# Attention outputs of a gated cross-attention layer by Strassen's method over pairs of token tiles

## The chip, the cores and the metric

The kernel runs on one core of a Trainium2 chip. The metric is the device time of one execution in microseconds (us), as the median of several runs. A core has TensorE (PE, matrix multiplications and transposes), VectorE (DVE), ScalarE (ACT), GpSimd (POOL) and SyncE (SP, which issues DMAs), each with its own queue of instructions, which it works in order. PE writes to PSUM, which consists of banks of 512 floats in each of 128 partitions; DVE and ACT read the results from there.

## The reference

Everything is f32. A batch has 4 sequences of 1024 tokens with 512 features, 16 heads and 64 context rows per sequence.

```python
x = x + jnp.tanh(g_xattn[0]) * xattn(_layernorm(x), ctx_1024, ctx_1024, w_q, w_k, w_v, w_o)
x = x + jnp.tanh(g_ffn[0]) * ffn(_layernorm(x), w_gate, w_up, w_down)
# xattn
scores = jnp.einsum('bhqd,bhkd->bhqk', q, k) * SCALE       # causal mask added
weights = jax.nn.softmax(scores, axis=-1)
out = jnp.einsum('bhqk,bhkd->bhqd', weights, v)
return out.transpose(0, 2, 1, 3).reshape(bsz, q_len, HEADS * HEAD_DIM) @ w_o
# ffn: act_qdq rounds to 16 bits with one scale for the whole tensor, lpbq_dequant to 4 bits in blocks of 32
up = act_qdq(x @ lpbq_dequant(w_up).T)
gate = act_qdq(x @ lpbq_dequant(w_gate).T)
gate = act_qdq(gate * fixed_qdq_u16(jax.nn.sigmoid(gate)))
return act_qdq(gate * up) @ lpbq_dequant(w_down).T
```

The inner width of the feed-forward part is 1536. Only the attention part and the order of some weight preparation are touched by the change.

## The kernel before, in words

The 4096 tokens are 32 tiles of 128 tokens. Since the context has only 64 rows per sequence, the kernel folds the projections into two matrices per sequence: `m_all` (512 x 1024: key side times w_q, so that the scores of all heads are normalised x times it) and `vwo` (1024 x 512: value side times w_o, so that the attention output is the turned softmax weights times it). They are made in a setup stage of about 78 us; those of the sequences 2 and 3 go to DRAM and are fetched back later.

The attention stage is a loop over 16 pairs q of token tiles, four pairs to a sequence (about 78 to 560 us). A pair of its body does the following.

- It computes the scores of the next pair (`scores`, L524) by Strassen's method: seven products of a 2 x 2 block split, in which the two tiles are the block rows, instead of eight. Each product is two accumulating matmuls of 128x512, which the profile shows as four records (L536), in the three PSUM banks sp, sq, sn; ACT copies (L547, L553) and DVE additions (L542) put them together. The left factors' sums are made by DVE in `score_left` (L329), the right factors' sums once per sequence by DVE in `score_sums` (L347).
- `softmax` (L569) of these scores: a maximum (L580) and its negative (L590) on DVE, 16 exponentials per tile on ACT (L592, with a row sum each), the reciprocal (L597) and the product with it (L598) on DVE.
- `weights_turned` (L602) turns this pair's weights by PE transposes (L610) and ACT copies (L612).
- `renormed` (L631) takes tiles of two pairs earlier, whose attention is done: second layer norm (L637), maximum (L640), transposes (L645), copy on ACT (L646).
- `attend` (L615): per tile eight accumulating matmuls of 128x512 (one for each 128 of the contraction), which show as 16 matmul records (L621), as every f32 matmul here shows as two; then one DVE instruction x1 = tanh(g)*po + x (L627), a DMA of x1 to DRAM on POOL's queue (L628) and statistics for the second layer norm (L629).

From tile 16 on, chunks of w_gate are dequantized on DVE (`dequantized`, L211 to L222) and turned on PE (`turned_chunk`, L226), 12 chunks in 16 tiles (`gate_at`, L659). In the last eight tiles eight chunks of w_up are dequantized too, and turned behind the loop. Then come the gate stage (24 units of about 12.5 us), the up stage and the down stage, all of them with Strassen products; the gate stage dequantizes the four other chunks of w_up.

PE executes in the order in which the program is written (`tc.manual_schedule`). The order on the other engines is made by a scheduler from priorities, which follow the program's order; `tc.high_priority(SOON)` puts an instruction ahead. The built program's queues are then fixed. Big buffers are 20 slots of 8 KB; PSUM is three banks for scores, two for attention (`ps_o`, L521) and three for transposes (`ps_tr`).

Of the kernel before, what the change touches and what calls it, by code (L numbers as in the profile page):

```python
# [7 lines left out]
F32 = mybir.dt.float32  # L8
# [9 lines left out]
P = 128  # L18
# [9 lines left out]
def kernel(  # L28
# [38 lines left out]

    nc = tc.nc
# [30 lines left out]
    UPE = 8  # L99
# [165 lines left out]
    LO, HI = slice(0, HC // 2), slice(HC // 2, HC)  # L265
    add, sub = ALU.add, ALU.subtract
# [78 lines left out]
    score_right, t4m = {}, []  # L345

    def score_sums(b):  # L347


        m0, m1 = m_all[b]  # L350
        b11, b21, b12, b22 = m0[:, LO], m0[:, HI], m1[:, LO], m1[:, HI]
        t12 = slot([P, 2, HC // 2, H], f"t12m{b}")
        if b % 2 == 0:
            t4m.append(slot([P, 2, HC // 2, H], f"t4m{b // 2}"))
        t1, t2, t4 = t12[:, 0], t12[:, 1], t4m[-1][:, b % 2]
        score_right[b] = {1: b11, 2: b21, 3: b22, 4: t4, 5: t1, 6: t2, 7: b12}
        nc.vector.tensor_tensor(t1, b12, b11, sub)
        nc.vector.tensor_tensor(t2, b22, t1, sub)
        yield
        nc.vector.tensor_tensor(b12, b22, b12, sub)  # L360

        nc.vector.tensor_tensor(t4, b21, t2, sub)
        yield

    with tc.tile_pool(name="su", bufs=1) as su, tc.tile_pool(
# [130 lines left out]
        for a in reversed(range(B // 2)):  # L496
            if a == 0:
                for _ in score_sums(0):
                    pass
            for hp in range(HP):  # L500
                for b in (2 * a, 2 * a + 1):
                    ps = ps_mm.tile([P, H], F32, name=f"ps_vo{b}_{hp}", tag="mm")
                    for j in range(2):
                        half = slice(j * D, (j + 1) * D)
                        to = j if b % 2 == 0 else 1 - j
                        nc.tensor.matmul(
                            ps[to * D : (to + 1) * D, :], vT[half, hp, b * KL : (b + 1) * KL],
                            wo[hp // 4][half, hp % 4, :], start=True, stop=True,
                        )
                    dst = vwo[b][hp // 4][:, hp % 4, :]  # L510
                    if b % 2 == 0:
                        nc.scalar.copy(dst, ps)
                    else:
                        nc.vector.tensor_copy(dst, ps)
                    if b > 1 and hp % 4 == 3:
                        nc.gpsimd.dma_start(out=vwo_d[b][hp // 4], in_=vwo[b][hp // 4])


    xT = [None] * NTB
    with tc.tile_pool(name="ps_s", bufs=1, space=PSUM) as ps_s, tc.tile_pool(  # L520
        name="ps_o", bufs=2, space=PSUM  # L521
    ) as ps_o, tc.manual_schedule(engines={mybir.EngineType.PE}):

        def scores(q, then):  # L524


            a, b = left.pop(q), score_right[q // QPB]
# [5 lines left out]

            def prod(k, at, start):
                for h in range(HC // 2):
                    nc.tensor.matmul(  # L536
                        bank[at], a[k][:, h, :], b[k][:, h, :],
                        start=start and h == 0, stop=h == HC // 2 - 1, skip_group_check=True,
                    )

            def summed(dst, at, other):
                nc.vector.tensor_tensor(dst, bank[at], other, add)  # L542

            m1, c12, c22 = c[:, 1, 0], c[:, 0, 1], c[:, 1, 1]
            prod(1, "sp", True)
            with tc.high_priority(SOON):
                nc.scalar.copy(m1, bank["sp"])  # L547
            prod(6, "sq", True)
            with tc.high_priority(SOON):
                summed(c12, "sq", m1)  # L550
            prod(2, "sp", False)
            with tc.high_priority(SOON):
                nc.scalar.copy(c[:, 0, 0], bank["sp"])  # L553
            prod(7, "sq", False)
            with tc.high_priority(SOON):
                summed(c22, "sq", m1)
            prod(5, "sn", True)
            with tc.high_priority(SOON):
                summed(c22, "sn", c22)
            prod(4, "sq", False)  # L560
            with tc.high_priority(SOON):
                summed(m1, "sq", m1)
            then()
            prod(3, "sn", False)
            with tc.high_priority(SOON):
                summed(c12, "sn", c12)
# [35 lines left out]
        def weights_turned(t, e):  # L602

            ef = e[:, t % 2].rearrange("p h k -> p (h k)")
            eT = pa.tile([P, HP, P], F32, name=f"eT{t}", tag="eT")
            for q in range(HP // 4):
                ps = ps_tr.tile([P, 4, P], F32, name=f"ps_e{t}_{q}", tag="tr")
                for j in range(4):
                    hp = 4 * q + j
                    nc.tensor.transpose(ps[:, j, :], ef[:, hp * P : (hp + 1) * P], ident)  # L610
                with tc.high_priority(SOON):
                    nc.scalar.copy(eT[:, 4 * q : 4 * q + 4, :], ps)  # L612
                yield eT

        def attend(t, eT):  # L615

            b = t // TPB
            g, i = divmod(t, GRP)
            po = ps_o.tile([P, H], F32, name=f"po{t}", tag="po")
            for hp in range(HP):  # L620
                nc.tensor.matmul(  # L621
                    po, eT[:, hp, :], vwo[b][hp // 4][:, hp % 4, :],
                    start=(hp == 0), stop=(hp == HP - 1),
                )
            x1 = xg[g][:, i, :]
            with tc.high_priority(SOON):
                nc.vector.scalar_tensor_tensor(x1, po, tanh_g[0], x1, ALU.mult, ALU.add)  # L627
            nc.gpsimd.dma_start(out=x1_d[t], in_=x1)  # L628
            stats(pa, x1, mv2[:, t, :], f"b{t}")  # L629
# [26 lines left out]
        sg_t, ag, early_up = [], [], []  # L656
        last = NT - GRP

        gate_at = [NT // 2 + oc * (NT // 2) // IC for oc in range(IC)]  # L659
        gate_raw = {}  # L660
# [6 lines left out]

        two = centred(1)
        ahead = scores(0, lambda: next_left(1))
        softmax(0, ahead)  # L670
        for q in range(NQ):
            b, k = divmod(q, QPB)
            e = ahead
            if q % 2 == 0 and q // 2 + 2 < NG:
                load_group(q // 2 + 2)

            if b + 1 < B:
                if b > 0 and k == 0:
                    fetched(m_all[b + 1], m_d[b + 1], f"mb{b + 1}")
                if b > 0 and k == QPB - 1:  # L680
                    fetched(vwo[b + 1], vwo_d[b + 1], f"vb{b + 1}")
                if k == 1:
                    sums_ahead = score_sums(b + 1)
                if k in (1, 2):
                    next(sums_ahead)
            if q + 2 < NQ:
                two = centred(q + 2)
            if q + 1 < NQ:
                ahead = scores(q + 1, lambda: next_left(q + 2))
                softmax(q + 1, ahead)  # L690
            turns = [weights_turned(2 * q + i, e) for i in range(2)]
            next(turns[0])
            for i in range(2):
                t = 2 * q + i
                eT = next(turns[i])
                if q > 1:
                    renormed(t - GRP)
                if t in gate_at:
                    oc = gate_at.index(t)
                    turned_chunk(ps_tr, gate_raw.pop(oc), oc, wgT, "g")  # L700
                if i == 0:
                    next(turns[1])
                attend(t, eT)
                if t + AHEAD in gate_at:
                    oc = gate_at.index(t + AHEAD)
                    w = pa.tile([P, H], F32, name=f"w_g{oc}", tag="wraw", bufs=4)
                    dequantized(pa, w_gate[oc * P : (oc + 1) * P, :], w, f"g{oc}", oc < 4)
                    gate_raw[oc] = w
                if t >= NT - UPB:
                    ag.append(weight_sums(wgT, sg_t, t - (NT - UPB), "g"))  # L710

                if t >= last - GRP:
                    oc = t - (last - GRP)
                    if oc % GRP == 0:
                        w4 = slot([P, GRP, H], f"w_eu{oc // GRP}")
                    w = w4[:, oc % GRP, :]
                    dequantized(pa, w_up[oc * P : (oc + 1) * P, :], w, f"eu{oc}")
                    early_up.append(w)
                for c, d in ((0, 2), (2, 3), (3, 4)):
                    if t == last + d - 1:  # L720
                        w = slice(last + c, last + d)
                        rstd_of(pa, [(rstd2[:, w], mv2[:, w, 1])], f"c{c}")
# [8 lines left out]
        renormed(last + 1)  # L731
        renormed(NT - 2)
        for w in early_up[:-2]:
            up_chunk(ps_tr, w)
        renormed(NT - 1)
        for w in early_up[-2:]:
            up_chunk(ps_tr, w)
# [4 lines left out]
    with tc.tile_pool(name="praw", bufs=RAW) as praw, tc.tile_pool(  # L742
# [82 lines left out]
        with tc.tile_pool(name="pb", bufs=2) as pb, tc.tile_pool(  # L825
# [79 lines left out]
            w4 = slot([P, IC - UPE, H], "w_u4")  # L905
            ready = []
            for at, v in enumerate(tp * UPB + p for tp in pairs for p in range(UPB)):
# [5 lines left out]
                if at < IC - UPE:  # L913
                    oc = UPE + at
                    w = w4[:, at, :]
# [366 lines left out]
    def pair_steps(q, a):  # L1282
# [46 lines left out]
        LEFT, RIGHT = slice(0, HH), slice(HH, H)  # L1329
# [98 lines left out]
```

## Time and profile before

The time of the kernel is 1474.39 us (median of three runs, 1473.55 to 1474.7).

| | us |
|---|---|
| profiled execution | 1473.96 |
| its span | 1472.1 |
| PE busy | 1441.3 (98%) |
| DVE busy | 1090.3 (74%) |
| ACT busy | 639.4 (43%) |
| POOL busy | 95.5 (6%) |
| attention matmuls L621 (512 records, 593 ns mean) | 225.1 |
| exponentials L592 (480 records, 335 ns mean, without the reading of the sums) | 159.5 |

The profile is one execution. "Busy" is time in which an engine has an instruction in work; PE's instructions overlap, so that the mean duration of a matmul is longer than the distance between two starts, and it is this distance that counts. A timeline line gives start, duration, engine, line, output and inputs, the number of instructions taken together, and in brackets the idle time before the first of them with what ended it. The granted clock is 1.00 where TensorE runs at full speed.

### The profile page before, as it was taken

To read this page: it belongs to the slowest core of one execution; us is meant where nothing else is said; L and a number is where in the kernel's file an instruction comes from. 1 tells how busy PE (TensorE), PEld (TensorE's weight loads), DVE (VectorE), ACT (ScalarE), POOL (GpSimd) and SP (SyncE) were. 2 spreads that over 40 slices of the span, in tenths; PEclk is the share of its full clock that TensorE was granted. 3 is DMA by queue.
4 is the path that set the end of the run, shared out by engine and by line. 5 is a ranking of instruction groups with operands and counts; after the bars stand their busy time and mean duration, and the time that the engine had idled before them with its cause. 6 is when DMAs were issued, how large, how long until landed. Compare 5 with 4: busy or idle time off the path is not lost. (4 is left out here: it accounts for less than half of the span.)

```text
span 1472.1 us, 14498 instructions
## 1 busy us (share of the span) xinstructions
PE 1441.3 (98%) x4656; PEld 793.1 (54%) x4656; DVE 1090.3 (74%) x1986; ACT 639.4 (43%) x1653; POOL 95.5 (6%) x189
## 2 busy tenths in 40 slices
PE   8999999999999999999999999999999899999999
PEld 6544445444555454444444444444444448888887
DVE  3875657668777888999755569988888897666632
ACT  2536645655556663110011039977776432222200
POOL 0100000000000001000000000000000101111110
PEclk9999999999999999999999999999999999999999
DMA  8521212302122135652322439968557375555321
GB/s 300 226 90 51 79 71 72 136 32 75 51 104 70 77 130 210 247 218 101 138 85 99 159 115 337 374 231 304 211 213 268 144 292 182 186 186 174 141 72 43
DMA packets 71476, 231.67 MB, mean 157 GB/s; under 512 B 7268, under 2 KB 7524, under 8 KB 65892
## 3 DMA queue, kind: packets, MB, share of 16 engines
q1 hardware_dynamic: 46212, 131.09, 25.2%
q0 software_dynamic: 18272, 74.46, 13.0%
q10 hardware_dynamic: 6912, 25.17, 4.2%
q8 instruction: 36, 0.59, 0.2%
q14 instruction: 44, 0.36, 0.1%
HBM read 123.74 MB, written 106.95 MB: 157 GB/s over the span
## 5 line engine op out<-in xcount | busy, mean ns | idle before, releaser
L592 ACT ACTIVATE e<-e,mx 128x64 f32<-128x64 f32 x480 | 159.5, 335 | 12.6 <-DVE mx L590 12.5
L621 PE MATMUL po<-vwo,eT 128*128 128x512 f32 x256 | 112.6, 593 | 0.0
L621 PE MATMUL po<-vb,eT 128*128 128x512 f32 x256 | 112.5, 592 | 0.0
L765 PE MATMUL pqup<-t,wuT 128*128 128x512 f32 x192 | 92.4, 604 | 4.9 <-DVE raw_up L786 2.1
L592 ACT ACTIVATION_READ_ACCUMULATOR e<-e,mx 128x1 f32 x480 | 90.5, 189 | 0.0
L765 PE MATMUL pqgate<-t,wgT 128*128 128x512 f32 x192 | 90.4, 593 | 0.0
L781 ACT COPY raw_gate<-ppgate 128x512 f32<-128x512 f32 x24 | 14.1, 586 | 147.7 <-PE ppgate L765 147.7
L1294 PE MATMUL ep<-wdT,upe 128*128 128x256 f32 x336 | 77.1, 379 | 0.0
L621 PEld LDWEIGHTS po<-vwo,eT 128*128 128x128 f32 x256 | 47.4, 190 | 53.7 <-issue 53.6
L621 PEld LDWEIGHTS po<-vb,eT 128*128 128x128 f32 x256 | 47.4, 190 | 53.6 <-issue 53.6
L1220 ACT ACTIVATE uie<-upe,inv_up 128x1024 int16<-128x1024 f32 x48 | 53.6, 1145 | 46.4 <-DVE upe L1224 24.2
L1294 PE MATMUL eq<-tw,upe 128*128 128x256 f32 x312 | 72.4, 379 | 0.0
L1294 PEld LDWEIGHTS ep<-wdT,upe 128*128 128x128 f32 x336 | 63.8, 190 | 9.1 <-issue 0.5
L993 ACT ACTIVATE gi<-gt,inv_gate 128x1024 int16<-128x1024 f32 x48 | 54.9, 1143 | 30.6 <-DVE q L1003 30.3
L765 PE MATMUL ppgate<-xh,wgT 128*128 128x512 f32 x144 | 67.7, 592 | 0.0
L765 PE MATMUL ppup<-xu,wuT 128*128 128x512 f32 x144 | 67.7, 592 | 0.0
L765 PEld LDWEIGHTS pqup<-t,wuT 128*128 128x128 f32 x192 | 34.6, 189 | 57.1 <-issue 29.7
L1294 PEld LDWEIGHTS eq<-tw,upe 128*128 128x128 f32 x312 | 59.3, 190 | 8.1
L1224 DVE SCALAR_TENSOR_TENSOR upe<-uie,inv_o,gse 128x1024 f32<-128x1024 int16 (+1 forms) x50 | 60.5, 1235 | 3.0 <-ACT uie L1220 2.7
L765 PEld LDWEIGHTS pqgate<-t,wgT 128*128 128x128 f32 x192 | 36.2, 190 | 46.4 <-issue 38.5
L542 DVE TENSOR_TENSOR e<-sq,e 128x512 f32<-128x512 f32 x48 | 33.0, 688 | 36.8 <-PE sq L536 36.7
L893 DVE TENSOR_REDUCE am_gate<-raw_gate 128x1 f32<-128x1024 f32 x48 | 58.2, 1212 | 0.9
(330 smaller groups left out, 2881.6 us busy)
## 6 DMA issues: line engine op xcount, KB each, us to landing
gate_d<-raw_gate ACTq DMA_DIRECT2D x48, 512.0 KB, 2.6
gt<-gate_d SPq DMA_DIRECT2D x48, 512.0 KB, 4.7
upe<-up_d SPq DMA_DIRECT2D x24, 1024.0 KB, 6.5
up_d<-raw_up POOLq DMA_DIRECT2D x46, 512.0 KB, 3.6
gse<-gsi_d SPq DMA_DIRECT2D x24, 512.0 KB, 4.0
gsi_d<-q SPq DMA_DIRECT2D x44, 256.0 KB, 4.0
xg<-in_x_dram SPq DMA_DIRECT2D x8, 1024.0 KB, 6.3
x_d<-xg POOLq DMA_DIRECT2D x32, 256.0 KB, 2.3
```

What stands on the lines that cost most here:

```text
L542: nc.vector.tensor_tensor(dst, bank[at], other, add)
L592: nc.scalar.activation(ei[:, h, :], ei[:, h, :], AF.Exp, bias=mx[:, h : h + 1], accum_out=sm[:, h : h + 1],)
L621: nc.tensor.matmul(po, eT[:, hp, :], vwo[b][hp // 4][:, hp % 4, :], start=(hp == 0), stop=(hp == HP - 1),)
L765: nc.tensor.matmul(bank[at], a[k][:, h, :], b[k][:, h, :], start=start and h == 0, stop=h == HC // 2 - 1, skip_group_check=True,)
L781: nc.scalar.copy(r0[:, 0, :], bank["pp"])
L893: nc.vector.tensor_reduce(am_gate[:, u : u + 1], rf, AX.X, ALU.max, apply_absolute_value=True)
L993: nc.scalar.activation(gi, g, AF.Copy, scale=inv_g)
L1220: nc.scalar.activation(ui, up[:, i, :], AF.Copy, scale=inv_u)
L1224: ins = nc.vector.scalar_tensor_tensor(o[:, i, w], ui[:, w], c_o, gs[:, i, w], ALU.mult, ALU.mult)
L1294: nc.tensor.matmul(bank[at], a[u // 2][k][:, u % 2, q % 2, :], w_of[u // 2][k][:, u % 2, :], start=start and u == 0, stop=u == UPB - 1, sk ...
```

## The change

The attention output of a pair is now computed by Strassen's method as the scores are: the weights of the two tiles are the block rows, the contraction (1024) and the output width (512) are halved. Seven products of four program matmuls (56 records of 128x256) take the place of two tiles of 16 records of 128x512.

- The left factors' sums (four additions of 128x512 per pair) are made by POOL in `weights_turned`, which now turns a pair at a time, between the score products.
- The right factors' sums of `vwo` are made once per sequence by `batch_sums`, which replaces `score_sums`; all of them run on POOL, but for the scores' first.
- The tanh factor is multiplied into `vwo` when it is copied out of PSUM.
- The first product is copied by ACT (r); the others are added by DVE in 128x256 quarters straight to the two tiles of x, and POOL adds r to the other quarters. Two of the three accumulators are halves of one PSUM tile ("opn"), the third has a bank.
- The score products are done in the order 1, 6, 2, 5, 7, 3, 4 with the turning of weights behind 5 and 3.
- Gate chunks are turned from tile 20 on, two per pair ahead of `attend` in pairs 10 to 13, and the last four behind the loop; four early up chunks instead of eight are made ready in the loop, and the gate stage makes eight. The loads of tile groups are issued later in the body, and sums of gate weights start two tiles later.

```diff
-    UPE = 8
+    UPE = 4
@@
+    def batch_sums(b, k, engine):
+        if k == 0:
+            m0, m1 = m_all[b]
+            b11, b21, b12, b22 = m0[:, LO], m0[:, HI], m1[:, LO], m1[:, HI]
+        else:
+            v0, v1 = vwo[b]
+            b11, b12, b21, b22 = (v[:, :, h] for v in (v0, v1) for h in (LEFT, RIGHT))
...
+        engine.tensor_tensor(t1, b12, b11, sub)
+        engine.tensor_tensor(t2, b22, t1, sub)
         yield
-        nc.vector.tensor_tensor(b12, b22, b12, sub)
-        nc.vector.tensor_tensor(t4, b21, t2, sub)
+        engine.tensor_tensor(b12, b22, b12, sub)
+        engine.tensor_tensor(t4, b21, t2, sub)
         yield
@@
-                        nc.scalar.copy(dst, ps)
+                        nc.scalar.activation(dst, ps, AF.Copy, scale=tanh_g[0])
                     else:
-                        nc.vector.tensor_copy(dst, ps)
+                        nc.vector.tensor_scalar(dst, ps, tanh_g[0], None, ALU.mult)
@@
-        name="ps_o", bufs=2, space=PSUM
+        name="ps_o", bufs=1, space=PSUM
@@
+        def weights_turned(q, e):
+            eT = pa.tile([P, 7, HP // 2, P], F32, name=f"eT{q}", tag="eT", bufs=1)
+            for i in range(2):
+                ef = e[:, i].rearrange("p h k -> p (h k)")
+                for k in range(2):
+                    ps = ps_tr.tile([P, 4, P], F32, name=f"ps_e{q}_{i}_{k}", tag="tr")
...
                 with tc.high_priority(SOON):
+                        nc.scalar.copy(eT[:, 2 * i + k], ps)
...
+            a11, a12, a21, a22, s1, s2, s4 = (eT[:, k] for k in range(7))
+            nc.gpsimd.tensor_tensor(s1, a21, a22, add)
+            nc.gpsimd.tensor_tensor(s2, s1, a11, sub)
+            nc.gpsimd.tensor_tensor(a21, a11, a21, sub)
+            made.append(nc.gpsimd.tensor_tensor(s4, a12, s2, sub))
+            yield {1: a11, 2: a12, 3: s4, 4: a22, 5: s1, 6: s2, 7: a21}
+
+        def attend(q, a):
...
+            for k, at, start, dst in (
+                (1, "op", True, None), (6, "oq", True, x1[:, RIGHT]), (2, "op", False, x1[:, LEFT]),
+                (5, "on", True, x2[:, RIGHT]), (7, "oq", False, x2[:, RIGHT]),
+                (3, "on", False, x1[:, RIGHT]), (4, "oq", False, x2[:, LEFT]),
+            ):
+                for h in range(HP // 2):
+                    nc.tensor.matmul(
+                        bank[at], a[k][:, h, :], b[k][:, h, :],
+                        start=start and h == 0, stop=h == HP // 2 - 1, skip_group_check=True,
+                    )
                 with tc.high_priority(SOON):
-                nc.vector.scalar_tensor_tensor(x1, po, tanh_g[0], x1, ALU.mult, ALU.add)
+                    if k == 1:
+                        nc.scalar.copy(r, bank[at])
+                    else:
+                        nc.vector.tensor_tensor(dst, bank[at], dst, add)
+                if k == (6 if last else 3):
+                    engine.tensor_tensor(x1[:, RIGHT], x1[:, RIGHT], r, add)
+                if k == (2 if last else 4):
+                    v = x2.rearrange("p (n h) -> p n h", n=2)
+                    engine.tensor_tensor(v, v, r.unsqueeze(1).to_broadcast([P, 2, HH]), add)
...
+                behind = {3: lambda: next_left(q + 2)}
+                if q > 0:
+                    behind = {5: turn, 3: lambda: (a.append(turn()), next_left(q + 2))}
+                ahead = scores(q + 1, behind)
                 softmax(q + 1, ahead)
...
+            for t in (2 * q, 2 * q + 1):
+                oc = t - gate_from
+                if 0 <= oc < IC - 4:
+                    turned_chunk(ps_tr, gate_raw[oc], oc, wgT, "g")
+            attend(q, a[0])
+            if b + 1 < B and k in (1, QPB - 1):
+                with tc.issue_after(made[-1].ins):
+                    for _ in batch_sums(b + 1, k // 2, nc.gpsimd):
+                        pass
```

## The prediction

> **What bounds the kernel now.** I read, in this order, the engine totals, the table of stretches, the order of TensorE's work in one pair of token tiles, and then what the other engines hold ready for it. "L" numbers are lines of the kernel before, "A" numbers lines of the changed one.
>
> ```profile
> PE 1441.3 (98%) x4656; PEld 793.1 (54%) x4656; DVE 1090.3 (74%) x1986; ACT 639.4 (43%) x1653; POOL 95.5 (6%) x189
> ```
> ```profile
> 200.00:300.00 100.00, 99.84 (x309) 49.31 (x308) 66.82 (x137) 63.67 (x287) 4.90 (x10) 1.00 0.28 103
> ...
> 400.00:500.00 100.00, 99.99 (x339) 51.76 (x339) 82.33 (x177) 58.41 (x240) 3.79 (x7) 1.00 0.23 82
> ```
>
> In the second fence the columns are length, PE, PEld, DVE, ACT, POOL busy, then the granted clock. The pairs run from about 78 to 560 us; in these stretches PE is never idle, so less PE work is worth its full time, and so is each new PE wait, because no other slack stands ahead of it. DVE is at 67 to 82 of 100 and ACT at 55 to 64: both have room on average, but each works its queue strictly in order.
>
> ```profile
> 245.00 1.88 PE L536 MATMUL sq<-m_all,xs 128*128 128x512 f32 x4
> ...
> 251.02 1.88 PE L536 MATMUL sn<-m_all,xs 128*128 128x512 f32 x4
> 252.74 1.04 PE L610 MATMUL ps_e<-ident,e 128*128 128x128 f32 x8
> 253.61 0.60 PE L645 MATMUL ps_xm<-ident,xm 128*128 128x128 f32 x4
> 254.08 0.66 PE L610 MATMUL ps_e<-ident,e 128*128 128x128 f32 x4
> 254.57 7.03 PE L621 MATMUL po<-vwo,eT 128*128 128x512 f32 x16
> ```
>
> Starts give the prices, since PE's ends overlap: a score product (4 matmuls) is 252.74-251.02 = 1.72 us; 8 transposes 253.61-252.74 = 0.87; 16 attention matmuls end 6.87 us after they start (261.44-254.57), 0.429 each of 512 columns. An attention tile in before needs one DVE instruction after it, and two PSUM buffers alternate, so that nothing on PE waits for it.
>
> ```profile
> 256.67 0.35 ACT L592 ACTIVATE e<-e,mx 128x64 f32<-128x64 f32 x1 [1.18 <-DVE mx L590]
> 257.01 0.33 ACT L592 ACTIVATE e<-e,mx 128x64 f32<-128x64 f32 x1
> ```
> ```profile
> 261.64 0.75 DVE L627 SCALAR_TENSOR_TENSOR xg<-po,tg,xg 128x512 f32<-128x512 f32 x1 [4.94 <-PE po L621]
> 262.31 0.24 DVE L597 RECIPROCAL rs<-sm 128x16 f32<-128x16 f32 x1
> ...
> 263.04 1.21 DVE L598 TENSOR_TENSOR e<-e,rs 128x1024 f32<-128x1024 f32 x1
> ...
> 267.89 0.25 DVE L597 RECIPROCAL rs<-sm 128x16 f32<-128x16 f32 x1 [3.56 <-ACT e L592]
> ```
>
> The exponentials run one per 0.333 us, 16 per tile: 5.33 us, both tiles 10.7. DVE stands still for 3.56 us at 267.89 for the last of them. Today nothing on PE is behind that; this is the place to watch.
>
> **The saving.** Attention goes from 2x16 matmuls of 512 columns per pair to 7x8 of 256. A 256-column matmul in the down stage (L1294) starts every 0.216 us (12 in 2.59 us). So 56x0.216 = 12.09 us for 32x0.429 = 13.74: 1.65 us per pair, x16 pairs = -26.5 us. The transposes stay. Four fewer early up chunks at the end (16 transposes, 1.7 us) return in the gate stage, and cancel.
>
> **What moves off or on.** DVE per pair: six additions from PSUM of 128x256 (0.422 each, L1326) for two of 0.748: +1.0 us. The per-batch score sums leave DVE (4x1.22 for three batches, -14.6 us in all). ACT: one more 128x256 copy, 0.37 (L1308). The tanh scale goes into the copies of the value matrices: nothing, they run on ACT and DVE either way. Four more dequantizations of about 2.85 us go into the gate stage: 11.4 us of DVE, behind 24 units of 12.5 us of PE there; weights were ready 7 us or more ahead of use, so 0, and at most 11.4 without that cover. SP's loads of the next two tile groups are issued a pair later, but their slots are read a pair after that still: 0.
>
> **New waits on PE.** Let T be the end of score product 3. After T the changed order has 8 transposes of the second weight tile, 8 of the next x, score product 4 and 8 transposes of the renormalized tiles: attention starts at T+0.87+0.87+1.72+0.87 = T+4.33, its products (each 1.73) end at 6.06, 7.78, 9.51 and so on.
> (1) Products 2 and 5 are in the two halves of one PSUM tile ("opn"), and the built program has the first matmul of product 5 wait for DVE's reading of product 2 just before. DVE starts some 0.2 after the last matmul, needs 0.42, PE restarts 0.1 later: 0.7 us, in each pair: 11.5 us. With nothing else ahead in DVE's queue that is the whole loss.
> (2) Something is ahead in it. In the changed order of DVE, on odd pairs the reciprocal (A591) and the 1.22 us product (A592) of the first tile stand before that reading. Their exponentials can start at T+3.1 (the score row's maximum and ACT's four copies of 0.59 go first), take 5.33 and share ACT with the new copy (0.37): reciprocal done at T+9.1, product 6's reading 0.42, A592 1.22, the reading 0.42: 11.2, against 9.51 on PE: 1.7, or 2.6 where the mask's 1.2 us comes first, 2.9 in pair 1. I take 2.2 for pairs 3, 5, 7, 9. On even pairs a 0.68 maximum (A671) comes between: 1.0 to 1.6, I take 1.3 (with a 1.28 us table load on ACT). Pairs 1 to 9: 2.9+4x2.2+4x1.3 = 16.9.
> (3) Pairs 10 to 13 carry two gate chunks each ahead of attention, not one in 1.33 tiles. The second chunk's transposes need a buffer of the three in "ps_tr", which ACT's copy of a renormalized tile frees (A677). In pairs 12 and 13 that copy is behind all 32 exponentials in ACT's queue: 3.1 (4.4 with the table load of pair 12)+10.7+0.6 = T+14.4 to 15.7, then 0.5 of transposes, against an attention start of T+5.2 with the chunks. That is 9.7 and 11, and with (1) and the dequantizations on DVE ahead of its readings 10.4 and 13. In pair 10 the second tile's reciprocal (after 32 exponentials) is ahead of product 2's reading: 8.9; in pair 11 dequantizations hold the exponentials up: 5.9. Below, these four cannot be under 20 us, unless ACT's exponentials are quicker than 0.333; above, DVE adds some 8.
> (4) The first pair (POOL's sums of the value matrices right before use) 2.7, pair 14 0.8, pair 15 2.5.
> Sum: 16.9+8.9+5.9+13+10.4+2.7+0.8+2.5 = 61.1, which includes (1). Before had 4.4 us of gaps in the pairs: +56.7.
>
> **POOL.** Per pair it gets four 128x512 additions of turned weights, one 128x256 and one 128x512 addition to x, and per batch eight of 128x1024. No POOL row of this kind exists. From below: DVE's 128x512 addition took 0.69 (L219). From above a page: the Trainium skill, GPSIMD Engine Reference, section Elementwise — side-by-side cycle accounting, has an addition of 2048 floats at 4497 ns, as an estimate 2.2 ns an element: 1.15 us. The second sum, s2, is for product 6. The copies end at about T+1.9: s2 is there at T+1.9+2x0.69 = 3.3 or T+1.9+2x1.15 = 4.2, and product 6 starts at 6.06. By either nothing is lost; I take the page's, no row of POOL being near. Against the change stands another rule, the Trainium skill, SBUF — State Buffer, section Who interferes with whom: a DVE instruction with two SBUF inputs and a POOL instruction that reads SBUF shut each other out. DVE's sums of x parts (4x0.418, L342) and its products e*rs (2x1.22) have two SBUF inputs and fall there. The row: POOL did 95.5 us in all before, mostly issuing DMAs, and shows nothing of it. By the row 0; by the rule a sum waits for one such instruction at most, 1.2 us each: s2 at 4.2+2x1.2 = 6.6, 0.5 us late, 8 us over 16 pairs. I take 0 for the likeliest, since most of DVE's work beside s2 reads PSUM or one input, and keep 8 for the range.
>
> **The clock.**
>
> ```profile
> 341.46 1.31 PE L335 MATMUL ps_xn<-ident,xn 128*128 128x128 f32 x8 [2.61 <-DVE xn L323]
> ```
> ```profile
> 341.00:352.00 11.00, 10.54 (x42) 6.23 (x43) 9.64 (x18) 5.94 (x14) 0.00 (x0) 0.84 0.08 25
> ```
> After a gap of 2.61 us the granted clock averaged 0.84 over 11 us: (1-0.84)x11 = 1.7 us lost (the matmul of four at 342.56 took 3.39 for 1.88). Gaps of 1.56 and 1.28 at 568 and 571 left it at 1.00. The Trainium skill, TensorE: Matmul & The Clock Gate, section "What's actually happening", has a free-running window of 3.4 us. A rule of 3.4 us idle would charge only pairs 10 to 13, 4x1.7 = 7; the row charges from 2.6 us on, some 6 gaps (those four, pair 1 and one of the odd ones), 6x1.7 = 10 us. By the rule the sum below would be 3 us less; I take the row's 10.
>
> **Sum.** 1474.0 (profiled execution; span 1472.1) -26.5+56.7+0.7 (end of attention: two chunks' sums behind the last tile)+10 = 1514.9. The median is 0.4 above the profiled execution: 1515.
>
> **Rivals.**
> (A) Faster: ACT and DVE run far enough ahead that only the 0.7 us bank wait stays. 1474.4-26.5+11.5-4.4 = 1455; with the clock untouched. It asks that the copies A677 in pairs 12 and 13 aren't behind the exponentials in time; deciding point: losses under 31 us in total. For it: DVE has 18 to 33% idle. Against: both queues' order is fixed.
> (B) Half the waits of (2) to (4) and little of the clock: 11.5+25-4.4-26.5+4 = +10 to +20: 1484 to 1495.
> (C) POOL is the bound: additions over 2.1 us each (or shut out by DVE) bring s2 past product 6's start (2x2.1+1.9 = 6.1). At 3 us each it is 1.8 late per pair, +29: 1544. Against: twice DVE's price is 1.4.
> (D) The saving isn't there: 256-column matmuls could stand on their weight loads (190 ns each, L1294). The down stage's 0.216 speaks against.
>
> **How the numbers follow.** Chance of the forecast (1500 to 1530) 0.50, B 0.25, C 0.15, A 0.08, D within the others 0.02. 1485 leaves out A and a little of B, 1548 the worse half of C. Faster by over 0.2% (about what a measurement of this kernel tells from no change) 0.08, within 0.02, slower 0.90.
>
> **What would show it.** In the trace after: A643 matmuls 0.216 us apart (saving); a PE gap of 0.7 us or more ahead of product 5 in each pair, released by DVE xg A651; 1.3 and 2.2 us alternating; gaps of about 10 us ahead of the gate transposes of pairs 12 and 13, released by ACT xT A677; clock under 1 after them; no gap released by POOL outside the first and last pairs. It is wrong if POOL's additions take over 2 us, or the gaps at pairs 10 to 13 are under 3 us.

## The result, and the profile after

The changed kernel takes 1563.62 us (median of 4 runs, 1561.32 to 1564.24) against 1473.97 for the kernel before (4 runs): 1.0608 times as long, 95% interval 1.0589 to 1.0626. The prediction, 1515 with a range up to 1548, had the direction and most of the places right, but less than half of the size: 41 us of 90.

The engine totals of the changed kernel, to be read against those of before:

```profile
PE 1444.9 (93%) x5040; PEld 882.7 (57%) x5040; DVE 1159.2 (74%) x2034; ACT 646.8 (41%) x1668; POOL 287.7 (18%) x311
```

PE's busy time did not fall although 26.5 us of matmuls left it, and its share is 93% where it was 98%. Two stretches of the changed kernel say why (columns: length, PE, PEld, DVE, ACT, POOL busy, granted clock, DMA share, GB/s):

```profile
200.00:300.00 100.00, 88.53 (x351) 60.19 (x350) 72.14 (x130) 53.04 (x230) 48.65 (x34) 0.97 0.22 79
...
400.00:500.00 100.00, 75.97 (x301) 52.38 (x299) 81.24 (x139) 48.18 (x208) 44.50 (x30) 0.87 0.20 74
```

PE stands still for 11 of 100 us in the one and 24 in the other, in stretches where it was idle for 0.2 us or less before, and the granted clock falls to 0.97 and 0.87 (1.00 before). Busy time at a lower clock counts as busy: that hides the saving in the totals.

The account of the attention stage: from the first score matmul to the first gate matmul the time grew from 489.7 us (78.40 to 568.09) to 578.0 (79.55 to 657.51), by 88.3 us. I added up PE's gaps over 0.08 us in both: 7.0 before, 95.7 after. Without gaps this part is 482.7 and 482.3 us long, the same, although the saving of 26.5 and four up chunks (1.7) are gone from it. So something took back 28 us: 88.3 = 88.7 (gaps) - 28.2 (work) + 27.8. Most of it is the clock: 1 minus the granted clock, summed over the time in which PE works in this stage, is 25.4 us in the changed kernel's trace and 1.7 in the one before; some 4 us of the 27.8 stay unexplained.

One even pair of the changed kernel, PE's timeline (start, duration, instruction; in brackets the idle time before it and what ended it):

```profile
173.24 1.89 PE L643 MATMUL opn<-vwo,eT 128*128 128x256 f32 x8
174.97 1.89 PE L643 MATMUL oq<-t,eT 128*128 128x256 f32 x8
177.16 1.99 PE L643 MATMUL opn<-vwo,eT 128*128 128x256 f32 x8 [0.30 <-ACT r L649]
182.01 2.98 PE L643 MATMUL opn<-t,eT 128*128 128x256 f32 x8 [2.86 <-DVE xg L651]
184.78 2.64 PE L643 MATMUL oq<-vwo,eT 128*128 128x256 f32 x8
187.26 1.89 PE L643 MATMUL opn<-vwo,eT 128*128 128x256 f32 x8
```

The products are 1.73 us apart where nothing waits (174.97-173.24), as predicted. Product 5 (182.01) waits for DVE's reading of product 2, as predicted, but 2.86 us and not 1.3; then two products take 2.77 and 2.48 us, at a lower clock. What DVE did meanwhile:

```profile
171.76 0.46 DVE L341 TENSOR_TENSOR xs<-xs 128x256 f32<-128x256 f32 x1
172.14 1.24 DVE L584 TENSOR_SCALAR mx<-mx 128x16 f32<-128x16 f32 x1
173.30 1.56 DVE L325 TENSOR_SCALAR xn<-xg,mv,rstd 128x512 f32<-128x512 f32 x1
174.78 1.48 DVE L342 TENSOR_TENSOR xs<-xs 128x256 f32<-128x256 f32 x1
176.19 0.68 DVE L558 TENSOR_TENSOR e<-sq,e 128x512 f32<-128x512 f32 x1
```

and POOL beside it:

```profile
170.68 1.26 POOL L613 TENSOR_TENSOR eT<-eT 128x512 f32<-128x512 f32 x1 [9.75 <-ACT eT L609]
172.01 1.34 POOL L614 TENSOR_TENSOR eT<-eT 128x512 f32<-128x512 f32 x1
173.31 1.27 POOL L615 TENSOR_TENSOR eT<-eT 128x512 f32<-128x512 f32 x1
174.54 1.45 POOL L616 TENSOR_TENSOR eT<-eT 128x512 f32<-128x512 f32 x1
```

The negation of 16 maxima takes 1.24 us (0.17 when nothing runs on POOL, and in the kernel before, L590), the normalisation 1.56 (0.54), the sum of x parts 1.48 (0.42). Each ends within 0.3 us of the end of a POOL addition: 173.38 against 173.35, 174.86 and 174.58, 176.26 and 175.99. These are 3.1 us by which DVE is late for product 6 and product 2, and 2.1 of them are instructions with a single input (negation and normalisation).

DVE instructions that read one of two inputs from PSUM, and reductions (L574, 1.21 us with POOL at work and without), are not held up. One that runs wholly beside a POOL addition, DVE first, then POOL:

```profile
412.73 0.41 DVE L651 TENSOR_TENSOR xg<-opn,xg 128x256 f32<-128x256 f32 x1
```
```profile
411.68 3.33 POOL L369 TENSOR_TENSOR mb<-mb 128x1024 f32<-128x1024 f32 x1
```

Beside the sums made once per sequence (128x1024, 2.3 to 3.3 us on POOL) it is worse; here DVE in pair 11, while POOL makes such sums:

```profile
482.76 2.06 DVE L342 TENSOR_TENSOR xs<-xs 128x256 f32<-128x256 f32 x1
484.74 2.55 DVE L343 TENSOR_TENSOR xs<-xs 128x256 f32<-128x256 f32 x1
487.22 2.56 DVE L344 TENSOR_TENSOR xs<-xs 128x256 f32<-128x256 f32 x1
489.70 2.71 DVE L584 TENSOR_SCALAR mx<-mx 128x16 f32<-128x16 f32 x1
```

ACT's first exponential starts behind these at 492.50, the copy of product 1 (r), which is in ACT's queue behind four of the exponentials, at 493.85, and PE waited 11.50 us for it.

### The profile page after: what moved, and what is told of

Read it like the earlier page. It is cut to its first block, busy times and chain, and to the rows that moved or that the text cites. A ratio compares the mean times of both kernels' runs of the same rounds, so it can differ in the third digit from the quotient of the medians.

```text
span 1561.9 us, 15489 instructions
## 1 busy us (share of the span) xinstructions
PE 1444.9 (93%) x5040; PEld 882.7 (57%) x5040; DVE 1159.2 (74%) x2034; ACT 646.8 (41%) x1668; POOL 287.7 (18%) x311
## 3 DMA queue, kind: packets, MB, share of 16 engines
q0 software_dynamic: 18272, 74.46, 12.3%
## 5 line engine op out<-in xcount | busy, mean ns | idle before, releaser
L556 ACT COPY e<-sp 128x512 f32<-128x512 f32 x32 | 18.7, 584 | 153.4 <-PE sp L550 153.4
L643 PE MATMUL opn<-t,eT 128*128 128x256 f32 x128 | 42.1, 485 | 39.2 <-DVE xg L651 39.2
L1009 POOL DMA_DIRECT2D up_d<-raw_up x46 | 24.5, 532 | 257.0 <-ACT si L1042 116.6
L643 PE MATMUL oq<-t,eT 128*128 128x256 f32 x256 | 61.0, 381 | 3.3 <-POOL eT L614 3.3
L550 PE MATMUL sq<-t,xs 128*128 128x512 f32 x128 | 61.9, 607 | 0.5 <-DVE xs L342 0.5
L643 PE MATMUL opn<-vb,eT 128*128 128x256 f32 x192 | 50.4, 409 | 11.8 <-ACT r L649 11.8
```

What stands on the lines that cost most here:

```text
L550: nc.tensor.matmul(bank[at], a[k][:, h, :], b[k][:, h, :], start=start and h == 0, stop=h == HC // 2 - 1, skip_group_check=True,)
L556: nc.scalar.copy(dst, bank[at])
L643: nc.tensor.matmul(bank[at], a[k][:, h, :], b[k][:, h, :], start=start and h == 0, stop=h == HP // 2 - 1, skip_group_check=True,)
L1009: queue.dma_start(out=up_d[u], in_=raw[u])
```

## The experiments

Each is an edit of the changed kernel, whose time is 1563.62 us; ratios are to the kernel before, which ran beside each, with 95% intervals. In the text, "lock" is short for this: an instruction of DVE or POOL stands still while one of the other engine runs.

**POOL writes the sums without reading.** The sums of factors are left out and zeros stand in their place; POOL's additions to x stay, and read.

```diff
-            nc.gpsimd.tensor_tensor(s1, a21, a22, add)
+            nc.gpsimd.memset(s1, 0.0)
...
-        engine.tensor_tensor(t1, b12, b11, sub)
+        engine.memset(t1, 0.0) if engine is nc.gpsimd else engine.tensor_tensor(t1, b12, b11, sub)
```

> Leaves out the sums of factors on POOL (those of the turned weights, of the value matrices and of the later score matrices): POOL fills the same buffers with zeros instead, so it writes SBUF and does not read it; PE's order, and DVE's order in pairs 1 to 9, are as in the changed kernel. Theory of the lock (a DVE instruction with two SBUF inputs, or a copy-like one, stands still while a POOL addition runs): DVE's x sums return from up to 2.6 us to 0.42 and the negated maxima (A584) from 1.2-2.7 to 0.16, the gaps ahead of product 5 in pairs 1 to 9 fall from 2.9-4.9 us to 0.9-2.3, pair 11's gap of 11.5 to about 3, and the total by 9x2+9 of gaps and some 12 of clock: about 1525. Pairs 12 and 13 keep their 10 to 12 us. Theory of the queue order alone (what stands ahead of the readings costs what it cost before): DVE's durations and the gaps stay, 1555 to 1565.

Measured: 1503.51 us, ratio 1.0196 (1.0179 to 1.0213): 60 us less, some 22 more than expected. The groups of this kernel (busy us, mean ns, idle before):

```profile
L344 DVE TENSOR_TENSOR xs<-xs 128x256 f32<-128x256 f32 x16 | 6.7, 419 | 0.0
...
L584 DVE TENSOR_SCALAR mx<-mx 128x16 f32<-128x16 f32 x30 | 6.0, 201 | 0.4
```

and of the changed kernel:

```profile
L344 DVE TENSOR_TENSOR xs<-xs 128x256 f32<-128x256 f32 x16 | 15.2, 949 | 0.0
...
L584 DVE TENSOR_SCALAR mx<-mx 128x16 f32<-128x16 f32 x30 | 22.1, 736 | 0.4
```

In pairs 1 to 9, where DVE works the same instructions in the same order but for seven swaps of neighbours, it has its old durations back, and the gaps ahead of product 5 are 0.52 us in every even pair and 0.9 to 1.9 in odd ones, 9.2 us in nine pairs for 34.1. Pair 11's loss goes from 12 us to 1.4; pairs 12 and 13 keep 12.3 and 9.3. POOL's fills are also shorter than its additions (0.54 us against 1.3), but in these pairs PE waited for no POOL result in either kernel, and the 14 of DVE's x sums that ran beside a fill took 0.42 or 0.43 us all the same: for the instructions with two inputs in SBUF it is the reading that hurts. (The negation of maxima was held up by fills too, three times, for 0.3 us each.) This settles the lock as a cause; the order of the queues explains what is left.

**The order of the products.**

```diff
-                (5, "on", True, x2[:, RIGHT]), (7, "oq", False, x2[:, RIGHT]),
-                (3, "on", False, x1[:, RIGHT]), (4, "oq", False, x2[:, LEFT]),
+                (7, "oq", False, x2[:, RIGHT]), (5, "on", True, x2[:, RIGHT]),
+                (4, "oq", False, x2[:, LEFT]), (3, "on", False, x1[:, RIGHT]),
```

> Only the order of the attention products is changed, to 1, 6, 2, 7, 5, 4, 3, so that one product lies between each reading of a PSUM half and the product that needs it. Theory of the bank wait: each of 15 pairs gains up to 1.7 us of cover, the gaps of 2.9 to 4.1 ahead of product 5 shrink to 1.2 to 2.4, the granted clock is restored in those pairs (about 1 us each more): 1563 - 24 - 12, about 1525 to 1535. Rival (DVE is late as a whole, the wait only moves to the next product): 1555 to 1565.

Measured: 1538.93 us, ratio 1.0443 (1.0425 to 1.0460): 24.7 us less, where 28 to 38 were expected. Now each product waits for a reading two products back, so that 1.7 us of PE's own work covers it. In odd pairs waits of 1.3 to 1.4 us stayed ahead of product 5, and others moved to product 7 (0.4 to 1.8 us); on balance the gaps of the attention stage fell from 95.7 to 81.1 us, and its time without gaps from 482.3 to 468.6: half of the gain is clock (25.4 us lost in the changed kernel, 12.3 here).

**Gate chunks behind attention.**

```diff
-            for t in (2 * q, 2 * q + 1):
-                oc = t - gate_from
-                if 0 <= oc < IC - 4:
-                    turned_chunk(ps_tr, gate_raw[oc], oc, wgT, "g")
             attend(q, a[0])
+            for t in (2 * q, 2 * q + 1):
+                oc = t - gate_from
+                if 0 <= oc < IC - 4:
+                    turned_chunk(ps_tr, gate_raw[oc], oc, wgT, "g")
```

> Only the gate chunks of pairs 10 to 13 are turned behind attention instead of ahead of it. Theory (their transposes wait for ACT's copy of a renormalized tile, which is behind 32 exponentials): the gaps of 12.2 and 10.7 us in pairs 12 and 13 go, with 3 to 7 us of clock; pair 11's 11.5 us stays, since it comes from POOL's sums: about 1533 to 1540. Rival (the lateness moves to ACT's copy r or to the next pair): 1555 to 1565.

Measured: 1539.33 us, ratio 1.0443 (1.0425 to 1.0460): 24.3 us less. The gap that it removes, as the changed kernel's PE and ACT show it:

```profile
536.39 1.11 PE L227 MATMUL wps_g<-ident,w_g 128*128 128x128 f32 x4 [12.15 <-ACT xT L677]
```
```profile
535.45 0.33 ACT L586 ACTIVATE e<-e,mx 128x64 f32<-128x64 f32 x1
...
535.78 1.04 ACT L677 COPY xT<-ps_xm 128x512 f32<-128x512 f32 x2
```

The copy that frees the PSUM buffer comes right behind the last exponential, as the prediction said. In pairs 12 and 13 the chunks' waits are gone; 2.7 and 3.0 us ahead of products 2 and 5 come out in their place. The gaps of the stage fell by 24 us, the whole gain: the 3 to 7 us of clock that were expected with them did not come, but pair 11's wait, which was to stay, fell by 3 us.

**All sums of factors on DVE.**

```diff
-            nc.gpsimd.tensor_tensor(s1, a21, a22, add)
+            nc.vector.tensor_tensor(s1, a21, a22, add)
...
-                    for _ in batch_sums(b + 1, k // 2, nc.gpsimd):
+                    for _ in batch_sums(b + 1, k // 2, nc.vector):
```

> All sums of factors go from POOL to DVE, where they stand in its queue at 0.69 us (four per pair) and 1.22 us (eight per sequence). Theory of the lock: DVE loses about as much time to its own additions (2.75 us a pair) as it lost standing still for POOL's (2 to 3), so pairs without batch sums change little, and those with them gain some 2 us, pair 11 more: 1540 to 1560. If POOL were merely late with its results (its 1.3 us an addition on PE's path), the gaps would close: under 1530. If DVE's queue were the only trouble, four more instructions ahead of the readings would make it slower: over 1575.

Measured: 1514.53 us, ratio 1.0285 (1.0265 to 1.0305): 49 us less. My range for the lock, 1540 to 1560, was missed; the number falls into the one that I had set for a POOL that is merely late with its results. That isn't the cause all the same: in the changed kernel PE waited for a POOL sum in two pairs only, for 1.83 (pair 0) and 1.48 us (pair 15). With four more additions a pair in its queue DVE was still earlier than beside POOL: product 5 waited 0.9 to 1.8 us in pairs 1 to 9, not 2.9 to 4.9. The engine that was to be relieved is better off with the work: an addition costs it 0.68 us (L613) in its own queue, while POOL needs 1.3 us for it and can hold DVE up for all of that.

**Only the sums per sequence on DVE**, the pair's four stay on POOL (the second line of the diff above alone, and the same for the first sequence; as in that run, these sums no longer have to wait for the pair's).

> One part undone: the sums made once per sequence go from POOL to DVE (1.22 us each there), POOL keeps the four sums of turned weights. Theory of the lock: the odd pairs lose the part of their gaps that came with POOL's 2.3 to 3.3 us instructions (1 to 2 us each, with clock), pair 11's 11.5 us shrinks to 3 to 5: 1540 to 1550, and the even pairs keep 2.9 us each. Rival (eight more DVE instructions per sequence hold the readings up as long): 1560 or more.

Measured: 1562.47 us, ratio 1.0586 (1.0561 to 1.0611): no gain. Here my expectation fell and the rival's number held. Pair 11's gap did shrink, from 11.5 to 3.0, but others grew. The moved additions have two SBUF inputs themselves and now run beside POOL's four; in pair 3 (DVE, then POOL):

```profile
205.74 2.29 DVE L366 TENSOR_TENSOR t<-vwo 128x1024 f32<-128x1024 f32 x1
207.96 1.49 DVE L341 TENSOR_TENSOR xs<-xs 128x256 f32<-128x256 f32 x1
```
```profile
205.41 1.55 POOL L613 TENSOR_TENSOR eT<-eT 128x512 f32<-128x512 f32 x1 [9.10 <-ACT eT L609]
207.03 2.13 POOL L614 TENSOR_TENSOR eT<-eT 128x512 f32<-128x512 f32 x1
```

DVE's takes 2.29 us instead of 1.22, and POOL's second 2.13 instead of 1.34: it goes both ways. Only five of the 28 moved additions were slowed so; how much of the lost gain is theirs and how much the longer queue, as the rival had it, was not separated.

**Only the pair's sums without reading** (the first line of the first diff alone).

> Leaves out only the four sums of turned weights per pair, which POOL fills with zeros instead; the sums per sequence stay on POOL. It splits the 60 us that both together cost. Theory: the four sums lock DVE in all 15 pairs (3 us each), the sums per sequence only in 6 pairs: 35 to 45 of the 60 us, 1520 to 1528, and pair 11's gap stays at 8 us or more. If the sums per sequence did most of it, as pair 11's 2.6 us instructions suggest: 1540 or more.

Measured: 1546.23 us, ratio 1.0492 (1.0475 to 1.0510): 17 us less; the other 43 of the 60 us go only when the sums per sequence are left out as well. My split was the wrong way round. In six pairs their four long instructions, with only short fills ahead of them, start earlier and meet other instructions of DVE: its x sums take 1.09 us on average (L344; 0.95 in the changed kernel), and product 5 in pair 1 now waits 6.2 us (4.9 there). How the two parts share the 60 us depends on what they meet, so the parts don't add up (17, and 1 for moving the other), and I don't give either a price of its own.

**The edits together.** First the three that helped:

> The three edits together: all sums of factors on DVE, the product order 1, 6, 2, 7, 5, 4, 3, the gate chunks behind attention. If the gaps are independent, the run with the sums on DVE (1514.5) loses its 14 waits of 0.5 to 2.3 us ahead of product 5 (about 17) and pair 13's 9.3 and pair 10's 6.2 (12 or so of 15), with a few us of clock: about 1480. If DVE is the bound once it has all sums, the waits move on instead of going: 1500 or more.

Measured: 1492.16 us, ratio 1.0118 (1.0101 to 1.0135). The waits for readings are gone but for two (0.74 and 0.35 us); new ones stand in even pairs, ahead of transposes of x (L337) and of renormalized tiles (L676), up to 5.1 us. Then the gate chunks back in the places of the kernel before, the four sums with high priority:

> As the run before, and the gate chunks are dequantized and turned in the places of the kernel before (from tile 16 on, one in 1.33 tiles, the turning behind attention, none behind the loop), and the four sums of turned weights have high priority. Theory: what is left of the gaps are the setup's, the first pair's and those at the end of attention (12 to 15 us, about what before had), so that the whole saving of 26.5 us shows: 1448 to 1460. If 256-column matmuls or the extra DVE work cost something that is not a wait of these kinds: 1465 to 1480.

Measured: 1496.97 us, ratio 1.0158 (1.0141 to 1.0175): not better, and far from the 1448 to 1460 that were expected. Three gaps of 7.0 to 7.5 us ahead of x's transposes and one of 4.7 ahead of a renormalized tile's remain, where PE waits for DVE in even pairs. The same places and order with the sums left on POOL, at their old priority:

> POOL keeps all the sums; the product order and the places of the gate chunks are those of the run e6. The difference to e6 is what the sums on POOL cost once the queues are in order. Theory of the lock: DVE still stands still 3 us a pair and more beside the sums per sequence; 1.7 us of cover takes a part of it, so 20 to 40 us over e6: 1475 to 1495. If the lock only hurt through the bad order of the queues: within 5 us of e6.

Measured: 1517.91 us, ratio 1.0295 (1.0278 to 1.0312), 21 us over the run before it, the low end of what the lock was expected to cost: so much the sums on POOL cost with this better order of the queues. Then, back with the sums on DVE (but the first sequence's for the value matrices on POOL), the statistics of x a pair earlier and the early up chunks two tiles earlier:

```diff
             turns = weights_turned(q, ahead)
+            if q % 2 == 0 and q // 2 + 2 < NG:
+                load_group(q // 2 + 2)
...
+            if q % 2 == 0 and q // 2 + 2 < NG:
+                g = q // 2 + 2
+                group_stats(pa, g)
+                rstd_of(pa, [(rstd1[:, of_group(g)], mv1[:, of_group(g), 1])], f"a{g}")
             if q % 2 == 1 and q + 1 < NQ:
...
-                if t >= last:
+                if last - 2 <= t < NT - 2:
                     made_ready(early_up, UPE, w_up, "eu")
```

> As e6, with the next tile group loaded and its statistics and scale made one pair earlier (apart from those of the attention output), the value matrices' first sums on POOL, and the early up chunks two tiles earlier. e6 had four gaps of 4.7 to 7.4 us in pairs 4, 8, 10 and 12, where transposes of x waited for a chain of statistics on DVE. Theory: they are DVE's backlog at one place and go with it (26 us and some 8 of clock), and 3 us at the end: 1455 to 1465. If DVE has no room on average (it was busy 80 to 86 of 100), they move on: 1480 or more.

Measured: 1476.01 us, ratio 1.0013 (1.0006 to 1.0020), where 1455 to 1465 was expected. This kernel and the next don't compute the layer, and their times are not those of a usable kernel: with the early up chunks two tiles earlier, the last gate chunk is dequantized into the buffer of the up chunks, where the fourth up chunk overwrites it before it is turned, so that PE turns up weights for the gate. The trace of the next run shows the buffer's wrong name (w_eu under a gate scale, then turned as gate):

```profile
511.02 0.68 DVE L222 TENSOR_TENSOR w_eu<-w_eu,wam_g 128x512 f32<-128x512 f32 x1
```
```profile
551.69 0.60 PE L227 MATMUL wps_g<-ident,w_eu 128*128 128x128 f32 x4
```

The instructions are as many as in a right one, so the waits up to there can be read; what a right one takes was not measured. From 120 to 300 us PE has hardly a gap; three of 5.4 to 6.1 us stay, where attention waits for transposes of tiles that it doesn't need. Last, these transposes go behind it:

```diff
-            if q > 1:
-                for t in (2 * q, 2 * q + 1):
-                    renormed(t - GRP)
             attend(q, a[0])
+            if q > 1:
+                for t in (2 * q, 2 * q + 1):
+                    renormed(t - GRP)
```

> As e10, with the renormalized tiles' transposes behind attention instead of ahead of it, so that DVE's work on them has 12 us more. In e10 attention waited three times 5.4 to 6.1 us for them (pairs 8, 10 and 14). If these waits are a matter of place: 17 us and 3 of clock less than 1476, 1454 to 1460, faster than the kernel before by 1%. If DVE's backlog in these pairs is the cause, the wait moves to the readings or to the next pair's factors: 1468 to 1478.

Measured: 1468.49 us (6 runs), ratio 0.9966 (0.9954 to 0.9979): 0.3% under the kernel before, but with the wrong gate chunk, and at the edge of the range for a wait that moves on (1468 to 1478). The fastest kernel here that computes the layer is the one with the three edits together, 1492.16 us, 1.2% slower than the kernel before. One pair of the last run on PE:

```profile
219.19 1.89 PE L643 MATMUL opn<-vwo,eT 128*128 128x256 f32 x8
220.92 1.89 PE L643 MATMUL oq<-t,eT 128*128 128x256 f32 x8
...
229.55 1.89 PE L643 MATMUL opn<-vwo,eT 128*128 128x256 f32 x8
231.28 1.04 PE L676 MATMUL ps_xm<-ident,xm 128*128 128x128 f32 x8
```

Seven products in 231.28-219.19 = 12.09 us, to the hundredth what the prediction had; the run with the gate chunks in their old places, which does compute the layer, has the same in pair 12 (486.66 to 498.75). 23.8 us of gaps (7.0 before) and some 5 us more of clock loss keep the rest of the 26.5 us. 10 of those us are four waits of the gate chunks' transposes for ACT, 2.3 to 2.6 each; and DVE, busy 93.69 of 100 us from 300 to 400 in this kernel, leaves little room to order things better; whether more is to be had wasn't tried.

## Why the prediction was wrong, by its own steps

**The saving** was right: 12.09 us per pair, shown by the pairs above. Rival (D) falls, and so do (A) and (B), which asked for fewer and shorter gaps than forecast.

**The new waits** had the right places in pairs 1 to 9, 12 and 13. The idle time in front of attention's products and the transposes ahead of them, in us (predicted without the 4.4 us taken off for the kernel before):

| pairs | predicted | changed kernel | POOL writes only |
|---|---|---|---|
| 1 to 9 | 16.9 | 34.1 | 9.2 |
| 10 | 8.9 | 7.9 | 6.5 |
| 11 | 5.9 | 12.0 | 1.4 |
| 12 | 13 | 12.8 | 12.3 |
| 13 | 10.4 | 11.2 | 9.3 |

In pair 10 the size is near, but by luck: 5.2 of the 7.9 us stand ahead of x's transposes, not ahead of product 5. In pair 11 PE waited for the copy r behind DVE instructions held up by POOL, not for dequantizations. The end of the stage, 0.7 in the sum, has gaps of 3.65 and 4.20 us (0.52 and 1.56 before), of nearly this size in the run with fills too.

The last column shows two errors that partly hid each other. The queues' order alone (steps 1 and 2) costs half of what I took: the bank wait is 0.52 us, not 0.7, and even pairs have nothing beyond it. And the lock, which I took at 0, makes up the rest of the second column there: 25 us in nine pairs. Step 3, the chunks behind 32 exponentials, was right in pairs 12 and 13 to 1 us.

**The step that failed is the one on POOL**, where it says "I take 0 for the likeliest". It asked by how much DVE delays POOL's sum s2, found slack there, and kept 8 us for the range. It should have asked the other way round: by how much POOL delays DVE, which is on the path by then through its reading of product 2. The rule that I weighed, the Trainium skill, SBUF — State Buffer, section Who interferes with whom, was right against the row: it names as affected the DVE instructions with two SBUF inputs, and single-input ones like tensor_scalar in the two-port modes, in which DVE takes ports that it shares with POOL, while reductions are not. No trace shows the mode, but the trace has the effect on all three: L342 at 1.48 us, L584 at 1.24 with 16 elements to a row, the maximum L574 that ran beside POOL's first addition at 1.21 as always. So the reason given for the 0, that most of DVE's work beside s2 reads PSUM or one input, holds for PSUM and fails for one input. The page also says that a POOL instruction which only writes does not contend with two-input additions, which the run with fills shows: L344 0.419. That POOL was nearly idle in the trace of before meant only that its row could not speak on it. Removing POOL's reads (and shortening its work) is worth 60 us, more than the 49 by which the prediction missed; without them the time is under the forecast, 1503.51 for 1515.

POOL's own price was somewhat low: 1.15 us was meant as a bound from above (2.2 ns times 512 are 1.13), and the additions of 128x512 took 1.26 at least, 1.30 to 1.44 in the mean, 2.25 in one case beside DVE. As predicted, PE waited for a POOL sum only in the first pair and pair 15. So the measured time lies nearer to rival (C)'s 1544, but not for its reason: POOL's results were in time, and what cost was that DVE stood still beside it.

**The clock** cost more than twice the 10 us that I took. The count was wrong: I counted six gaps, since most odd and all even pairs were to stay below 2.6 us, and there are 16. The price of 1.7 us per gap was right for the short ones: seven drops of 3.41 us at half clock cost 1.4 to 1.7 us of PE's work each, but five about the long gaps of pairs 9 to 13 last 6.8 to 17.1 us and cost 1.6 to 4.5. That 16 times 1.7 makes 27, near the 28 of the account, is luck, for three of the 16 gaps cost nothing. Two stretches of the changed kernel, behind the gaps of 2.86 and 11.50:

```profile
182.00:185.00 3.00, 2.99 (x9) 2.47 (x10) 1.34 (x2) 3.00 (x21) 0.00 (x0) 0.65 0.00 0
...
494.00:499.00 5.00, 4.24 (x9) 2.98 (x10) 4.43 (x11) 5.00 (x31) 0.00 (x0) 0.50 0.00 0
```

Neither the row's 2.6 us nor 3.4 us idle is a limit, though: behind another gap of 2.86, at 314.11, the clock stayed at 1.00, and in the run with fills a gap of 1.89 at 201.94 was followed by half clock. The changed kernel, then the run with fills:

```profile
314.11:320.00 5.89, 5.89 (x27) 5.22 (x28) 2.74 (x7) 4.67 (x25) 0.00 (x0) 1.00 0.00 0
```
```profile
203.34:206.75 3.41, 3.41 (x9) 2.70 (x8) 0.68 (x2) 2.91 (x14) 0.20 (x1) 0.50 0.01 2
```

The traces tell the two apart. In each of them all drops begin whole multiples of 3.41 us apart (in the changed kernel at 182.88, 217.01, 380.85), which agrees with the free-running window that the prediction cites. I laid this grid over the attention stages of all 13 traces: each of the 101 windows at full clock that were followed by half clock had PE idle for 1.89 us or more of its 3.41, and none of the 1733 that were not had it idle for more than 2.00. The gap at 314.11 lies across two windows, 1.3 us in one and 1.5 in the other. So it is idle time in a window, about 1.9 to 2.0 us, and not the length of a gap that decided here.

**What moved at no cost** (the dequantizations into the gate stage, the tanh factor) stayed free: outside the attention stage the time changed by 89.7-88.3 = 1.4 us. Whether the later loads of tile groups cost nothing, as predicted, stays open: the last gain but one came from loading them and making their statistics earlier, with other things; how much of it is theirs wasn't separated.

## What to carry to other kernels

Before work goes to an idle engine, list what it shares with the busy one, and ask in both directions who stands still for whom: here a DVE instruction on 16 elements a row cost as much as the POOL addition beside it. A matmul saving on a full PE is only worth what the other engines' queues can keep up with: give each PSUM reading a product of cover, and keep work that attention doesn't need, and that hangs on late copies, behind it. Count the gaps of about 2 us and more as well as their sum, for many of them cost a second time, in clock.

## What the runs showed of the hardware that was not expected

A POOL addition held up DVE by its whole length, even an instruction of 0.17 us that came to take 2.71. Moving long additions from POOL to DVE beside other POOL additions gained nothing (1562.47), and where they met both were slower (2.29 for 1.22, 2.13 for 1.34). The two parts of POOL's work did not add up: without the reads of one 17 us, without those of both 60. The clock fell by PE's idle time within windows of 3.41 us: a gap of 1.89 us cost it, one of 2.86 across two windows did not.
